# A graph network on one core: another order of the head's text, and the last load of x in two parts

## The chip, the core and the metric

The kernel runs on one core of one Trainium2 chip. Five engines work side by side, each on its own queue of instructions, in order: TensorE (PE, matmuls), VectorE (DVE), ScalarE (ACT), GpSimd (POOL) and SyncE (SP, which here only issues transfers). They wait for each other by semaphores. Sixteen DMA engines move data between HBM and the on-chip memory (SBUF); a transfer is issued from the queue of SP, ACT or POOL. Matmuls write to banks of PSUM, from which ACT and DVE copy results away. The metric is the time of one execution on the device, in microseconds (us); lower is better.

## What is computed

```python
h = jnp.maximum(_layernorm(x, axis=-1), 0.0)     # x: 2500 x 256
xs = [h]
for W, b in ((W0, b0), (W1, b1), (W2, b2)):      # W: 512 x 256
    xi, xj = h[dst], h[src]                      # 80000 edges, sorted by dst
    m = jnp.concatenate([xi, xj - xi], axis=-1) @ W + b
    s = jax.ops.segment_sum(m, dst, num_segments=N)
    cnt = jax.ops.segment_sum(ones, dst, num_segments=N)
    h = relu(s / jnp.maximum(cnt, 1.0)[:, None])
    xs.append(h)
out = x + jnp.concatenate(xs, axis=-1) @ Wf + bf
```

## The kernel before

The kernel turns the sums over edges into products with a matrix of counts: how often node `src` sends to node `dst`. x's 2500 rows lie in 20 tiles of 128 rows, taken as 10 pairs (pair q is tiles 2q and 2q+1). The columns of the count matrix are cut in windows of 6 nodes, and windows in batches of 4. Five groups of windows make the columns of one layer; the first layer's products of group g run while the counts of group g+1 are made, and layers 1 and 2 read the counts back from HBM.

This case is about the **head**, some 60 us in which x is normalized, the first products are made, edges are gathered and the counts of group 0 begin. Everything in it goes through a wrapper (`InOrder`, line 282, which therefore is the line of nearly all records) that keeps each engine's instructions in the order in which the program names them. That order is written out by hand in a string, `order` (lines 914 to 924): each word names an act, with a number for its pair, group, batch or window of keys, and `perform` calls them one after the other. An act puts its instructions at the end of the queues of the engines it uses; so two words may change places without any effect if they share no engine, and a word moved past another of the same engine changes that queue. The acts that matter here:

| word | what it does | engine |
| --- | --- | --- |
| `st` q | mean and variance of pair q's tiles (2 bn_stats, 2 bn_aggr), from x in `acc` | DVE |
| `rs`, `sq`, `sc` g | for a group of pairs: variance + eps; its root; the scale `rs` and offset `off` | DVE; ACT; DVE |
| `N` q | normalizes pair q in place in `acc`: pair 0 on DVE and ACT, 1 on ACT, from 2 on POOL | as told |
| `T`, `R` q | four transposes into the bank `turned`; relu of it into `hT` | PE; ACT |
| `Z`, `F` q | the pair's product with W's lower half, with Wf's first block, in a bank `pz` (each recorded as 8 matmuls) | PE |
| `H`, `L` q; `G` q | Z split into a high part `zh` and a low part `zl`; F copied to `acc` | ACT, DVE; ACT |
| `V` 9 | adds the bias row to the last tile's Z | DVE |
| `pk`, `sg`, `se` | find where each window's edges start: product, count of signs, position `start_i` (`se0` for keys 0, `se1` for keys 1 to 3) | PE; ACT; DVE |
| `ge` i | two indirect gathers of edges by `start_i`: `ed` (from dst), then `es` (from src) | POOL |
| `ka` i | `lo_i` from `es` (DVE); `away` from `ed` (ACT); a filter on `away` (DVE) | DVE, ACT |
| `km`, `kb` i | key parts `km` from `lo_i`; `kn` from `es` and `away` (two DVE instructions) | ACT; DVE |
| `kt`, `k1`, `k2` i | the keys transposed; copied to `key_m` and `key_n` | PE; ACT |
| `B` b | compares of keys with a row of numbers, for batches b and b+1 (a word whose batch is there already does nothing): one `one_m`, two `one_n` | DVE |
| `C` b, `E` b | counts of batch b in a bank (8 small matmuls, so that two batches are shown as 16); copied to `a` | PE; ACT |

The groups for `rs`, `sq` and `sc` are pairs 0; 1; 2 and 3; 4 to 7; 8 and 9. So `rs1`, `sq1` and `sc1` need only `st1`, and `sc2` needs `st2` and `st3`. B0 does only batch 0; B1, B3, B5, B7 and so on do two.

x comes in four chunks of tiles, 0 to 1, 2 to 5, 6 to 11 and 12 to 19, into `acc`. ACT's queue issues dst and then the chunk 6 to 11. SP's queue issues x 0 to 1, x 2 to 5, W's lower half (`wbf`, read by Z), x 12 to 19 (in two transfers, as the last tile has 68 rows), Wf's first block (`wbf`, read by F), W's upper half (`wt`, read after the head) and two short bias rows. The banks of `C`, `kt` and `pk` come from a pool of two, those of `T` from one of two, those of `Z` and `F` from one of four.

Of the kernel before, what the change touches and what calls it, by code (L numbers as in the profile page):

```python
# [10 lines left out]
AF = mybir.ActivationFunctionType  # L11
# [302 lines left out]
def by_windows(ctx: ExitStack, tc: tile.TileContext, x, src, dst, Ws, bs, Wf, bf, out, missing):  # L314
    nc = tc.nc
    PE, DVE, ACT, POOL, SP = nc.tensor, nc.vector, nc.scalar, nc.gpsimd, nc.sync
    PEo, DVEo, POOLo, ACTo, SPo = (InOrder(tc, e) for e in (PE, DVE, POOL, ACT, SP))
# [3 lines left out]
    NT = (N + P - 1) // P  # L321
# [15 lines left out]
    N1 = NT * KEEP  # L337
# [45 lines left out]
    away = early.tile([P, WG, CAP], BF16, name="away")  # L383
# [12 lines left out]
    lim = const.tile([P, WG], F32, name="lim")  # L396
    below = const.tile([P, WG], F32, name="below")
# [28 lines left out]
    def load_x(queue, a, b):  # L426
        queue.dma_start(acc[:, a:min(b, NT - 1), :], xr[:, a:min(b, NT - 1), :])
        if b == NT:
            queue.dma_start(acc[:LAST, NT - 1, :], x[(NT - 1) * P:N, :])

    chunks = [(0, 2), (2, 6), (6, 12), (12, NT)]
    load_x(SPo, *chunks[0])
    load_x(SPo, *chunks[1])
    load_x(ACTo, *chunks[2])
# [6 lines left out]
    def new_raw(l):  # L441
        raws[l] = raw_pools[-1].tile([P, DC, 2, D], F32, name="wbf", bufs=1)
# [8 lines left out]
    def load_wt(l, queue=SP):  # L451
        queue.dma_start(wts[l] if l == 1 else ws[l][0], Ws[l][0:D, :].rearrange("(c p) d -> p c d", p=P))

    def load_wf(l, queue=SP):
        if l == L:
            new_raw(l)
        wfs[l] = raws[l][:, :, 1, :]
        queue.dma_start(wfs[l], Wf[l * D:(l + 1) * D, :].rearrange("(c p) d -> p c d", p=P))

    load_wb(0, SPo)  # L460
    load_x(SPo, *chunks[3])
    load_wf(0, SPo)
    load_wt(0, SPo)

    lim_i = pp.tile([P, WG], I32, name="lim_i")
# [45 lines left out]
    first = pp.tile([P, 1], F32, name="first")  # L511
    after = pp.tile([P, 1], F32, name="after")
    behind = pp.tile([P, WG * P], F32, name="behind")
    pick = pp.tile([P, WG * P], F32R, name="pick")
# [7 lines left out]
    edges = [None] * WG  # L522
# [47 lines left out]
    def search(i, j):  # L570
        sl = slice(i, j)
        DVEo.tensor_add(base[:, 0, sl], base[:, 0, sl], base[:, 1, sl])
        DVEo.tensor_scalar(start_f[:, sl], row[:, sl], float(R), float(HR + P * R - MORE - CAP), op0=OP.mult, op1=OP.add)
        DVEo.scalar_tensor_tensor(start_f[:, sl], base[:, 0, sl], -0.5, start_f[:, sl], op0=OP.mult, op1=OP.add)
        DVEo.tensor_scalar(start_i[:, sl], start_f[:, sl], 0.0, float(E - CAP), op0=OP.max, op1=OP.min)
# [17 lines left out]
    parts = {}  # L593

    def key_parts(i):
        es, ed = edges[i]
        lo_i = pw.tile([P, CAP], I32, name="lo_i")
        DVEo.tensor_scalar(lo_i, es, P - 1, None, op0=OP.bitwise_and)

        ACTo.activation(away[:, i, :], ed, AF.Relu, bias=below[:, i:i + 1])  # L600
        DVEo.scalar_tensor_tensor(away[:, i, :P], away[:, i, :P], most if i == 0 else float(KEEP), away[:, i, :P],
                                  op0=OP.is_le, op1=OP.mult)
        parts[i] = [lo_i]

    def key_low(i):
        km = pw.tile([P, CAP], BF16, name="km")
        ACTo.copy(km, parts[i][0])
        parts[i][0] = km
# [18 lines left out]
    def key_copy(i, q):  # L627
        n = min(P, NW - i * P)
        to = (key_m, key_n)[q]
        ACTo.copy(to[:, i * P:i * P + n, :, :].rearrange("p n j r -> p j n r"),  # L630
                  parts[i][:, q * CAP:(q + 1) * CAP].rearrange("p (j n) -> p j n", j=CH)[:, :, :n]
                  .unsqueeze(3).to_broadcast([P, CH, n, REP]))
# [226 lines left out]
    def layer(l, g, a, own, PE=PE, ACT=ACT):  # L859
# [41 lines left out]
        "dstr": lambda: ACTo.copy(dst_r[:, MORE:], dst_i),  # L901
        "pk": lambda i: pick_half(i // 10, i % 10), "sg": lambda i: count_half(i // 10, i % 10),
        "se": lambda i: search(*((0, 1), (1, WG))[i]), "ge": get_edges,
        "ka": key_parts, "km": key_low, "kb": key_high, "kt": key_turn,
        "k1": lambda i: key_copy(i, 0), "k2": lambda i: key_copy(i, 1),
        "io": small_numbers, "ws": lambda: DVEo.tensor_sub(ws[0][0], ws[0][0], ws[0][1]),
        "st": stats, "rs": lambda g: spread(*groups[g]), "sq": lambda g: roots(*groups[g]),
# [4 lines left out]
        "warm": keep_warm,  # L912
    }
    order = """
        warm8 lim io first next dstr st0 rs0 sq0 pick sc0 warm7 N0 pk00 sg00 pk01 st1 T0 pk11 R0 sg01 st4 rs1 sq1 Z0 pk30 se0
        sg11 sc1 pk20 N1 st5 sg30 ge0 T1 st6 R1 F0 sg20 pk21 st7 pk10 H0 F1 rs3 st3 sq3 sc3 G0 st9
        L0 sg21 N6 pk31 ka0 kb0 Z1 N5 st8 N7 G1 T6 rs4 sg10 sg31 km0 T5 se1 kt0 R6 H1 st2 F6 sq4 sc4 k10 k20
        rs2 Z6 ge1 L1 T7 B0 R5 R7 Z5 B1 C0 B2 ka1 G6 H6 N9 H5 C1 T9 F7 E0 ge2 kb1 R9 sq2 km1 E1 kt1 C2 B3 k21 Z9
        k11 N8 L6 B4 E2 L5 C3 B5 C4 T8 E3 E4 C5 V9 R8 E5 ge3 ka2 H9 sc2 Z7 H7 F8 G7 B6 N3 N2 ka3 km2 T2 R2 km3
        kb2 C6 T3 kb3 B7 L7 kt2 Z2 B8 B9 L9 E6 C7 k22 k12 kt3 H2 N4 E7 B10 k13 k23 Z8 L2 C8 T4 C9 E8  # L920
        C10 H8 E9
        F9 B11 B12 C11 G8 E10 C12 R4 E12 E11 B13 F5 B14 C13 R3 B15 C14 E13 E14 L8 B16 Z3 G9 B17 C15 C16 H3 E15
        G5 B18 F3 C17 E16 C18 F4 E17 B19 C19 Z4 L3 G3 B20 E18 C20 B21 F2 E19 B22 H4 E20 L4 G4 B23 G2 B24 ws
# [29 lines left out]
    C1 = 1.0 + 1.0 / E12  # L953
# [483 lines left out]
def gnn_kernel(tc: tile.TileContext, x, src, dst, Ws, bs, Wf, bf, out):  # L1437
    nc = tc.nc
    with tc.tile_pool(name="flag", bufs=1) as flag:
        missing = flag.tile([1, 1], I32, name="missing")  # L1440
        tc.mark_branch_hint_location("again", "LikelyTaken",
                                     engines=[getattr(mybir.EngineType, e) for e in ("PE", "DVE", "Activation")])
        near_end = by_windows(tc, x, src, dst, Ws, bs, Wf, bf, out, missing)
        loads, (again,) = nc.values_load_multi_w_load_instructions(missing, min_val=0, max_val=1)

        for d in loads:
            if d.ins.engine in [getattr(mybir.EngineType, e) for e in ("PE", "DVE", "Activation")]:
                tc.add_manual_dep(d.ins, near_end.ins.name,
                                  mybir.DependencyInfo(mybir.DependencyClass.Sync, mybir.DependencyReason.DATA),
                                  reason="behind the outputs")  # L1450
        with tc.If(again > 0, label="again"):
            general(tc, x, src, dst, Ws, bs, Wf, bf, out)
# [28 lines left out]
```

## Time and profile before

| | us |
| --- | --- |
| median of 3 runs | 473.46 (473.29 to 473.58) |
| the profiled execution | 473.55 |
| its span, first to last record | 471.7 |
| PE busy from 8 to 20, 20 to 37, 37 to 61, 61 to 470 | 11.12, 16.84, 23.61, 405.40 |
| DVE busy in the same | 10.79, 14.07, 22.42, 326.92 |
| granted TensorE clock, mean | 0.998 |

The profile records one execution: for each instruction its start, its duration and the engine. Views: a page with busy times and a span in 40 slices; the chain of work that ended last, followed back from the end to what released each step; the waits by engine, with what ended them; the timeline in order of time, in which equal neighbours are merged; and the transfers. Matmuls are pipelined: each starts before the one ahead has ended, so the distance of starts tells PE's pace. Times below are us from the start of the span.

### The profile page before, as it was taken

To read this page: it belongs to the slowest core of one execution; us is meant where nothing else is said; L and a number is where in the kernel's file an instruction comes from. 1 tells how busy PE (TensorE), PEld (TensorE's weight loads), DVE (VectorE), ACT (ScalarE), POOL (GpSimd) and SP (SyncE) were. 2 spreads that over 40 slices of the span, in tenths; PEclk is the share of its full clock that TensorE was granted. 3 is DMA by queue.
4 is the path that set the end of the run, shared out by engine and by line. 5 is a ranking of instruction groups with operands and counts; after the bars stand their busy time and mean duration, and the time that the engine had idled before them with its cause. 6 is when DMAs were issued, how large, how long until landed. Compare 5 with 4: busy or idle time off the path is not lost.

```text
span 471.7 us, 7365 instructions
## 1 busy us (share of the span) xinstructions
PE 463.1 (98%) x2739; PEld 365.6 (77%) x2739; DVE 380.3 (81%) x699; ACT 310.5 (66%) x543; POOL 43.2 (9%) x66
## 2 busy tenths in 40 slices
PE   8999999999999999999999999999999999999995
PEld 3787888787878878877887877876788788688685
DVE  7988988799898873499987847877899687578795
ACT  4876677686664542368769867874787798397540
POOL 2684014300101001000000000000000000000000
PEclk9999999999999999999999999999999999999999
DMA  8310083991823707532168551110212955220014
GB/s 277 92 54 3 1 164 64 189 215 30 164 58 69 153 0 149 128 97 77 48 217 317 190 175 40 50 45 1 88 44 83 347 188 195 88 89 0 1 62 159
DMA packets 21775, 52.07 MB, mean 110 GB/s; under 512 B 1943, under 2 KB 12134, under 8 KB 21734
## 3 DMA queue, kind: packets, MB, share of 16 engines
q1 hardware_dynamic: 14374, 33.41, 21.6%
q0 software_dynamic: 5856, 16.51, 18.3%
q10 hardware_dynamic: 1504, 1.63, 1.1%
q8 instruction: 22, 0.36, 0.3%
q14 instruction: 19, 0.16, 0.1%
HBM read 36.08 MB, written 15.46 MB: 109 GB/s over the span
## 4 chain that ended last, share of the span: by engine, by line
PE 88%; DVE 5%; POOL 3%; DMA 2%; issue 1%; ACTq 0%; DVEq 0%; POOLq 0%
PE bank L282 84%; PE pz L282 3%; DMA acc<-in_x_dram 2%; DVE acc L282 2%; POOL acc L282 1%; DVE st L282 1%; POOL ed L282 1%; POOL es L282 1%; DVE staged L282 1%; DVE tmp L282 0%; DVE zl L282 0%; DVE mv L282 0%; PE turned L282 0%; DVE kn L282 0%; DVE rs L282 0%
## 5 line engine op out<-in xcount | busy, mean ns | idle before, releaser
L282 ACT CAST block<-staged 128x1008 fp32r<-128x1008 bf16 x120 | 117.8, 1031 | 17.1 <-DVE staged L282 6.3
L282 PE MATMUL bank<-block,zh 128*128 128x504 f32 (+1 forms) x200 | 83.7, 419 | 0.0
L282 PE MATMUL bank<-a,zh 128*128 128x504 f32 (+1 forms) x200 | 81.7, 409 | 0.0
L282 ACT CAST a<-bank 128x480 fp32r<-128x480 f32 (+1 forms) x105 | 54.4, 561 | 38.6 <-PE bank L282 36.9
L282 PE MATMUL bank<-a,zl 128*128 128x504 f32 (+1 forms) x200 | 77.8, 389 | 0.0
L282 PE MATMUL bank<-block,zl 128*128 128x504 f32 (+1 forms) x200 | 77.3, 387 | 0.0
L282 DVE TENSOR_TENSOR one_m<-iota_m,key_m 128x2048 bf16<-128x2048 bf16 (+2 forms) x55 | 64.3, 1169 | 9.9 <-PE bank L282 9.7
L282 PE MATMUL bank<-block,sh 128*128 128x504 f32 x160 | 69.0, 431 | 0.0
L282 PE MATMUL bank<-block,staged 128*128 128x512 f32 (+1 forms) x288 | 63.5, 371 | 0.3 <-DVE staged L282 0.2
L282 PE MATMUL bank<-block,sl 128*128 128x504 f32 x160 | 62.6, 391 | 0.0
L282 PEld LDWEIGHTS bank<-block,staged 128*128 128x128 f32 x288 | 49.2, 188 | 11.4 <-DVE staged L282 1.6
L282 DVE TENSOR_TENSOR one_n<-iota_n,key_n 128x960 bf16<-128x960 bf16 (+2 forms) x110 | 51.5, 509 | 0.0
L282 DVE TENSOR_TENSOR block<-staged 128x1008 fp32r<-128x1008 bf16 x40 | 47.0, 1205 | 5.5 <-PE bank L282 4.3
L282 PEld LDWEIGHTS <-one_m 128*128 128x128 bf16 x834 | 37.4, 97 | 13.4 <-issue 7.5
L282 PEld LDWEIGHTS bank<-block,zh 128*128 128x128 f32 x200 | 37.6, 188 | 10.8 <-issue 2.5
L282 PEld LDWEIGHTS bank<-block,zl 128*128 128x128 f32 x200 | 37.6, 188 | 10.6 <-issue 3.5
L282 PE MATMUL bank<-one_n,one_m 128*128 128x120 bf16 x834 | 44.7, 204 | 0.0
L282 PEld LDWEIGHTS bank<-a,zh 128*128 128x128 f32 x200 | 37.8, 189 | 6.4 <-issue 0.2
L282 PEld LDWEIGHTS bank<-a,zl 128*128 128x128 f32 x200 | 37.8, 189 | 6.3 <-issue 0.2
L282 DVE TENSOR_TENSOR staged<-staged 128x1008 bf16<-128x1008 bf16 x40 | 27.2, 679 | 17.3 <-ACT block L282 16.9
L282 PE MATMUL pz<-wbf,hT 128*128 128x256 f32 x160 | 38.7, 387 | 0.2 <-ACT hT L282 0.2
L282 PEld LDWEIGHTS bank<-block,sh 128*128 128x128 f32 x160 | 30.1, 188 | 10.4 <-issue 3.5
(163 smaller groups left out, 617.7 us busy)
## 6 DMA issues: line engine op xcount, KB each, us to landing
staged<-a_dram SPq DMA_DIRECT2D x52, 504.0 KB, 4.5
a_dram<-a POOLq DMA_DIRECT2D x20, 630.0 KB, 10.3
acc<-in_x_dram POOLq DMA_DIRECT2D x3, 640.0 KB, 14.3
out_dram<-acc SPq DMA_DIRECT2D x15, 128.0 KB, 1.8
wbf<-in_L_gnn_Wf_dram SPq DMA_DIRECT2D x4, 256.0 KB, 12.6
acc<-in_x_dram SPq DMA_DIRECT2D x1, 896.0 KB, 9.9
acc<-in_x_dram ACTq DMA_DIRECT2D x1, 768.0 KB
wbf<-in_L_gnn_W_dram SPq DMA_DIRECT2D x3, 256.0 KB, 7.2
```

Of the source, the lines that this page charges most:

```text
L282: return self.tc.keep_in_program_order(call(*args, **kwargs))
```

## The change

Four things change, all in the head. The last chunk of x is cut in two, tiles 12 to 15 and 16 to 19, and Wf's first block is loaded between them. The ACT part of `ka` becomes an act of its own, `aw`, so that it can stand elsewhere than its DVE part. In the order, `st2` comes ahead of `rs1`, where `st4` stood, and `st4` goes behind `sc1`. And from the fourth line of the order on: `sc2` and `aw2` go to the place behind B4, `ka2` and `kb2` right behind `V9`, `aw3` and `km2` ahead of `Z7`, `C6` between `Z7` and `F8`, `ka3` and `kb3` ahead of `H7`, `N2` ahead of `N3`, and T2 and T3 come to stand together behind `F8`. After `C8` nothing is changed.

```diff
-    chunks = [(0, 2), (2, 6), (6, 12), (12, NT)]
+    chunks = [(0, 2), (2, 6), (6, 12), (12, 16), (16, NT)]
...
     load_wb(0, SPo)
     load_x(SPo, *chunks[3])
     load_wf(0, SPo)
+    load_x(SPo, *chunks[4])
     load_wt(0, SPo)
...
     def key_parts(i):
-        es, ed = edges[i]
+        es = edges[i][0]
         lo_i = pw.tile([P, CAP], I32, name="lo_i")
         DVEo.tensor_scalar(lo_i, es, P - 1, None, op0=OP.bitwise_and)
-
-        ACTo.activation(away[:, i, :], ed, AF.Relu, bias=below[:, i:i + 1])
         DVEo.scalar_tensor_tensor(away[:, i, :P], away[:, i, :P], most if i == 0 else float(KEEP), away[:, i, :P],
                                   op0=OP.is_le, op1=OP.mult)
         parts[i] = [lo_i]
+
+    def find_away(i):
+        ACTo.activation(away[:, i, :], edges[i][1], AF.Relu, bias=below[:, i:i + 1])
...
-        "ka": key_parts, "km": key_low, "kb": key_high, "kt": key_turn,
+        "aw": find_away, "ka": key_parts, "km": key_low, "kb": key_high, "kt": key_turn,
...
-        warm8 lim io first next dstr st0 rs0 sq0 pick sc0 warm7 N0 pk00 sg00 pk01 st1 T0 pk11 R0 sg01 st4 rs1 sq1 Z0 pk30 se0
-        sg11 sc1 pk20 N1 st5 sg30 ge0 T1 st6 R1 F0 sg20 pk21 st7 pk10 H0 F1 rs3 st3 sq3 sc3 G0 st9
-        L0 sg21 N6 pk31 ka0 kb0 Z1 N5 st8 N7 G1 T6 rs4 sg10 sg31 km0 T5 se1 kt0 R6 H1 st2 F6 sq4 sc4 k10 k20
-        rs2 Z6 ge1 L1 T7 B0 R5 R7 Z5 B1 C0 B2 ka1 G6 H6 N9 H5 C1 T9 F7 E0 ge2 kb1 R9 sq2 km1 E1 kt1 C2 B3 k21 Z9
-        k11 N8 L6 B4 E2 L5 C3 B5 C4 T8 E3 E4 C5 V9 R8 E5 ge3 ka2 H9 sc2 Z7 H7 F8 G7 B6 N3 N2 ka3 km2 T2 R2 km3
-        kb2 C6 T3 kb3 B7 L7 kt2 Z2 B8 B9 L9 E6 C7 k22 k12 kt3 H2 N4 E7 B10 k13 k23 Z8 L2 C8 T4 C9 E8
+        warm8 lim io first next dstr st0 rs0 sq0 pick sc0 warm7 N0 pk00 sg00 pk01 st1 T0 pk11 R0 sg01 st2 rs1 sq1 Z0 pk30 se0
+        sg11 sc1 pk20 N1 st4 st5 sg30 ge0 T1 st6 R1 F0 sg20 pk21 st7 pk10 H0 F1 rs3 st3 sq3 sc3 G0 st9
+        L0 sg21 N6 pk31 aw0 ka0 kb0 Z1 N5 st8 N7 G1 T6 rs4 sg10 sg31 km0 T5 se1 kt0 R6 H1 F6 sq4 sc4 k10 k20
+        rs2 Z6 ge1 L1 T7 B0 R5 R7 Z5 B1 C0 B2 aw1 ka1 G6 H6 N9 H5 C1 T9 F7 E0 ge2 kb1 R9 sq2 km1 E1 kt1 C2 B3 k21 Z9
+        k11 N8 L6 B4 sc2 aw2 E2 L5 C3 B5 C4 T8 E3 E4 C5 V9 ka2 ge3 kb2 R8 E5 H9 aw3 km2 Z7 N2 N3 C6 ka3 kb3 H7 F8 G7 B6 T2 R2
+        km3 T3 E6 B7 L7 kt2 Z2 B8 B9 L9 C7 k22 k12 kt3 H2 N4 E7 B10 k13 k23 Z8 L2 C8 T4 C9 E8
```

## The prediction

> **What bounds it.** I read the busy table first, then the slices, then the chain of waits in order of time, then the waits and the timeline of the first 48 us.
>
> ```profile
> PE 463.1 (98%) x2739; PEld 365.6 (77%) x2739; DVE 380.3 (81%) x699; ACT 310.5 (66%) x543; POOL 43.2 (9%) x66
> PE   8999999999999999999999999999999999999995
> ```
>
> TensorE (PE) is busy in all slices but the first and the last, and the chain is PE from 37.76 to 132 us (but for 0.02 us) and nearly so to the end. The work after the head is the same in both kernels, and from 61 to 470 us PE is busy for 405.4 of 409 us. So the change is worth what it moves the moment from which PE never waits again. That moment in the chain, and what stands ahead of it:
>
> ```profile
> 32.91 0.97 POOL es L282
> 33.88 1.34 issue
> 35.27 2.44 POOL acc L282 x4
> 37.76 0.44 PE turned L282 x2
> ...
> 41.00 0.05 PE bank L282
> 41.07 0.66 PE bank L282 x11
> ```
>
> The second half of T2 (`turned`) starts at 37.76 behind POOL's normalization (`acc`), and C7 at 41.07 behind the compare B7. The waits of the first 48 us (engine, waited for, total, times, longest):
>
> ```profile
> DVE st L282 <- DMA acc<-in_x_dram: 1.0, 1, 1.0
> ...
> PEld pz L282 <- DMA wbf<-in_L_gnn_Wf_dram: 0.2, 1, 0.2
> ```
>
> and of DVE from 20 to 42 us:
>
> ```profile
> DVE lo_i L282 <- DMA es<-in_src_dram,start_i: 1.4, 1, 1.4
> DVE away L282 <- ACT away L282: 1.3, 1, 1.3
> ```
>
> PE's timeline from 7.7 to 41 us is its queue's own work but for these holes: about 2 us up to 13.60 (it follows N0, N1 and Wf), 0.4 to 21 us, 0.8 to 0.9 around T2 (F8 ends near 36.8, T2's half waits to 37.76), 0.2 before C7 and 0.14 at C11 (16 matmuls took 0.80 where the others take 0.66). Some 1.2 us near the end is therefore within reach, and of the 2 us at the start only what is not lost again.
>
> **The change, part by part.**
>
> *st2 for st4 ahead of rs1.* DVE sat idle from 9.17 to 10.18, for x rows that come on ACT's queue. st2 (2 x 0.33 and 0.22: 0.87 us, the row of a pair of bn_stats) needs only rows that st1 already had, so it fills the hole. rs1, se0 and sc1 no longer stand behind the load but behind sg01 on ACT (ends 10.14): sc1 ends at 11.05 instead of 11.98. ge0 and N1 start 0.9 earlier (N1 on ACT 11.1 to 12.2). st4 now follows sc1, ends at 11.95, where sc1 ended before: from st5 to se1 DVE is where it was, and ge1 starts at 21.05 as before. st2's old place behind se1 (20.71 to 21.59) is empty: 0.87 us less DVE ahead of L1 and B0.
>
> *The loads.* SP's queue has one more issue (0.5 us by its rows; nothing on SP waits for issues before the `brow` rows). 384 + 68 KB no longer stand ahead of Wf; at the 299 to 350 GB/s of the windows from 8 to 14 us that is 1.3 to 1.5 us, and Wf, which landed at 13.60 (the wait), lands near 12.2. The Trainium skill, "DMA: Bandwidth & Descriptors", section "Anatomy of one DMA", speaks against splitting: about 2.0 us fixed for each DMA. By that sum Wf, one DMA later than need be, would gain nothing. The windows show transfers run without gaps (DMA share 1.03 to 1.11 from 4 to 14 us), so a fixed part lies beside other transfers; I take the 1.4. x's last rows land when Wf did, about 13.6; st9, their first reader, is at 15.85: hidden by 2 us, and the last load (wt) isn't read before the head's end.
>
> *PE with both.* F0 starts behind T1 at 12.45 instead of 13.60. F1, Z1, T6, T5 follow as before (N6 is done at 17.13, N5 at 18.4); kt0 has to wait for kn of kb0 (19.18): 19.3 for 20.20; F6 19.5 for 20.61. So PE is 1.1 us ahead from 19.5 on: Z5 23.5, T9 25.95, F7 26.4.
>
> *DVE and POOL, 21 to 33 us.* B0 starts at 21.70 (k20 ends 21.55), B1 at 22.94, ending 25.05 to 25.35. es1 lands about 25.1 (2.7 after its issue), ka1 at 25.2 for 26.07, B3 26.5 for 27.33. sc2 (0.35, from 34.80) now comes between L6 and L5, so B5 starts at 30.05 for 30.55 and ends at 32.15. C5's last matmuls read B5: C5 ends at 32.45 for 33.12. **That cuts PE's lead to 0.67**: most of what the loads gave is lost again here.
>
> POOL shares something with DVE's compares:
>
> ```profile
> 26.57 1.03 POOL L282 DMA_INDIRECT ed<-in_dst_dram,start_i  x1 [0.16 <-issue]
> 27.90 1.49 POOL L282 DMA_INDIRECT es<-in_src_dram,start_i  x1 [0.30 <-issue]
> ...
> 30.67 1.94 POOL L282 DMA_INDIRECT ed<-in_dst_dram,start_i  x1 [0.16 <-issue]
> 32.91 0.97 POOL L282 DMA_INDIRECT es<-in_src_dram,start_i  x1 [0.30 <-issue]
> ```
> ```profile
> 27.33 1.22 DVE L282 TENSOR_TENSOR one_m<-iota_m,key_m 128x2048 bf16<-128x2048 bf16 x1
> 28.47 0.97 DVE L282 TENSOR_TENSOR one_n<-iota_n,key_n 128x960 bf16<-128x960 bf16 x2
> ...
> 30.55 1.22 DVE L282 TENSOR_TENSOR one_m<-iota_m,key_m 128x2048 bf16<-128x2048 bf16 x1
> 31.69 0.97 DVE L282 TENSOR_TENSOR one_n<-iota_n,key_n 128x960 bf16<-128x960 bf16 x2
> ```
>
> An indirect issue takes 0.97 alone; the two that began inside a one_m ended 0.92 after that one_m did (28.47, 31.69). Both tell that it stands still until the running compare ends. The Trainium skill, "SBUF — State Buffer", "Who interferes with whom", has the exclusive port of DVE and GpSimd, but says (as an inference) that a tensor_tensor doesn't stall the writing of descriptors. By that, moving compares would cost or give nothing at the issues; by the rows, an issue that begins inside one_m loses up to 1.2 us. I go by the rows, and every edit of DVE's times re-rolls these meetings. Laid out: es1 22.31 to 23.3 (was 23.31); N9 behind B1 to 25.7 (was 26.41); ed2 25.85; es2 27.15, held by B3 to 28.6 (was 29.39); N8 to 29.75; ed3 at 29.9 against B5's one_m at 30.05. If it begins first it ends at 30.9, es3 at 32.15; if not, 32.15 and 33.4 (was 33.88). es3's edges land 2.6 after: 34.75 or 36.0, was 36.5.
>
> *aw2, kb2, aw3 earlier.* Away2 held DVE 1.35 us (33.24 to 34.59); at its new place on ACT (29.4 to 29.85, ed2 landed about 29.2) it is done before DVE comes, and kb2 goes with it into the time before es3. Two ACT rows (0.5) move ahead of E2; C4 waits for E2's bank and still starts unhindered (E2 ends 30.35, C4 at 30.8). aw3, ahead of km2, H7, G7 and R2 in ACT's queue, waits for ed3's landing (2.36 after its issue ends: 34.97 less 32.61) at 33.3 to 34.5; R2 must be done at 37.5 and is, at 36.9 plus 0.6. If ed3 landed 1 us later still, R2 would be late. From es3's landing to B7 there remain lo_i, away, hi_i, kn: 1.45 us, where it was 2.17 (kb2's 0.75 is gone). B7 starts at 36.2 or 37.45, was 38.72.
>
> *sc2 early, C6 between Z7 and F8, T2 and T3 together.* N2, now ahead of N3 as T2 is of T3, and N3 no longer wait for sc2 (1.39): they run behind ge3, to 34.5 or 35.8. Z7 32.45, C6 34.25 (E4 is done), F8 34.6, T2 36.4, T3 36.9 to 37.35, both without a wait; kt2 at 37.35 for 38.83, Z2 37.6 to 39.4. C7 needs B7's end (start plus 2.2): 38.4 or 39.65. C7 at 39.4 or 39.65 for 41.02.
>
> **The sum.** Lead carried to C5's end 0.67, T2's stall 0.81, C7's 0.15, C11's 0.14: 1.75 at most; 1.35 where ed3 meets B5. After C7 both PE and DVE keep their distance, and nothing there waits. The meeting is a toss, and small excess waits on the way are likelier than none: I take 1.4. Span 471.7 - 1.4 = 470.3, and the 1.85 us around the span (profiled execution 473.55) give 472.15; the median of the runs lies 0.09 lower, so **472.1**.
>
> **The rivals.**
>
> 1. *The gate stays.* POOL's chain gains nothing, es3 lands at 36.5 as before; then only kb2's 0.75 is gone: B7 37.97, gain 0.77, **472.7**. For it: every POOL time above depends on a meeting. Against it: B1 and B3 end 0.85 earlier.
> 2. *The loads do nothing* (Wf lands no earlier, F0 at 13.60). PE comes to C5 as before, then 0.81, 0.15 and 0.14 remain: **472.4**. For it: the fixed cost above. Against: gapless transfers.
> 3. *Slower.* es1 (22.31) no longer begins 0.16 before B0 but inside it. If the compares keep the port from one to the next, as they kept N9's second half (24.18 to 26.41, 2.23 us for 0.55) through all of B1, es1 issues only at 25.05 and lands at 27.75: ka1 1.7 late, B3 at 29.0, B5 32.6, C5 ends 35.0 for 33.12. Of these 1.9 us the 0.81 at T2 and some 0.15 come back: +0.95, **474.4**. It decides from the point where es1 is held over 0.9 us. For it: N9's row. Against: es2 and ed3 did get in between one_m and one_n.
> 4. *Nothing*: another wait between 41 and 60 us takes the lead back, **473.5**; DVE is full there, but ahead.
>
> **Chances.** Forecast 0.50, rival 1 0.18, rival 2 0.10, rival 3 0.17, rival 4 0.05. About 0.2% (0.95 us) is what a measurement of this kernel can tell from no change. Faster by more: 0.49 of the forecast, 0.08 of rival 2, 0.03 of rival 1: 0.60. Slower by more: most of rival 3, 0.14. The rest, 0.26, within. The forecast's own range is 471.6 to 472.6; with the rivals 471.4 to 474.2 leaves out no more than the ends of rival 3 and gains over 2 us.
>
> **What would show it.** F0 at 12.4; se1 at the same time as before; B0 0.8 earlier; es1's issue about 1.0 us long (rival 3: over 2); C5's end 0.7 earlier; no wait of PE for POOL at T2; B7 at 36 to 37.5; PE at C7 1.4 to 1.6 ahead and so at the first `bank<-a,zh` (60.89 now). I am wrong if es3 lands after 36.5, if ACT stands at aw3 past 35.5, or if the lead at C7 is gone at 61 us.

## The result, and the profile after

| | before | after | after, timed again |
| --- | --- | --- | --- |
| median of the runs, us | 473.40 (473.20 to 473.58) | 471.70 (471.29 to 472.05) | 472.28 |
| ratio to before, 95% interval | | 0.9965 [0.9955, 0.9975] | 0.9977 [0.9968, 0.9986] |
| the profiled execution, its span | 473.55, 471.7 | 472.05, 470.2 | 472.28, 470.4 |

The changed kernel is faster, by 1.7 us in one timing and 1.3 in the other (there before took 473.54). The profiled execution took 472.05, where the sum gave 472.15. Such totals are too coarse for terms of 0.2 us: dst and x land some tenths earlier or later from one execution to the next, and the 410 us behind the head, which is the same code, took 410.8 before and 410.6 and 410.4 in two executions after. (That scatter lies in the tail: up to the start of PE's last matmul they took 405.51, 405.50 and 405.46.) So all that follows reads three starts on PE: the first `pk` (the first `bank<-dst_r,pick`), Z7 (the first `pz` behind C5), and the first `bank<-a,zh`. I call the time from `pk` to Z7 stretch A and that from Z7 to `bank<-a,zh` stretch B. Two executions of the changed kernel gave 25.13 and 25.09 for A, 26.84 and 26.81 for B, within 0.05 us of each other. Run 12 will show 0.13 in A that none of its edits explains, so a difference under 0.15 in these sums is not read as a gain. From `pk` on the change is worth 1.20 or 1.27 us, near the 1.3 of the second timing; the rest of the first timing's 1.7 is not explained by these rows.

| | A | B | A + B | against before |
| --- | --- | --- | --- | --- |
| before | 25.40 | 27.77 | 53.17 | |
| after | 25.13 | 26.84 | 51.97 | 1.20 less |
| forecast (most, sum of its terms) | 24.73 | 26.67 | 51.40 | 1.77 less |

The busy table of the changed kernel, and its chain of waits in order of time (start, us, what; only the longest pieces):

```profile
PE 462.6 (98%) x2739; PEld 365.7 (78%) x2739; DVE 380.8 (81%) x699; ACT 310.7 (66%) x543; POOL 41.4 (9%) x66
```
```profile
30.38 1.13 DVE one_m L282
31.51 0.90 DVE one_n L282 x2
32.45 0.44 PE bank L282 x7
32.89 1.81 PE pz L282 x8
...
36.84 0.87 PE turned L282 x8
37.96 1.99 PE pz L282 x8
```

PE's busy share has not moved; what moved is where the chain goes over to PE for the rest of the head: at 32.45 (C5), out of DVE's compare B5, where before it was at 37.76 (T2), out of POOL. T2 and T3 now run as one piece. PE's timeline of the same place (start, us, what, count):

```profile
32.13 0.75 PE L282 MATMUL bank<-one_n,one_m 128*128 128x120 bf16 x8
32.73 1.97 PE L282 MATMUL pz<-wbf,hT 128*128 128x256 f32 x8
34.53 0.49 PE L282 MATMUL bank<-one_n,one_m 128*128 128x120 bf16 x8
34.86 1.97 PE L282 MATMUL pz<-wbf,hT 128*128 128x256 f32 x8
36.67 1.04 PE L282 MATMUL turned<-shift,acc 128*128 128x128 f32 x8
37.55 0.28 PE L282 MATMUL bank<-ident_b,km 128*128 128x128 bf16 x2
37.66 0.28 PE L282 MATMUL bank<-ident_b,kn 128*128 128x128 bf16 x2
37.96 1.99 PE L282 MATMUL pz<-wbf,hT 128*128 128x256 f32 x8
39.79 0.49 PE L282 MATMUL bank<-one_n,one_m 128*128 128x120 bf16 x8
```

The reader is to see four things. C5 (32.13) takes 0.75 where a batch takes 0.49: PE has caught up with DVE's B5. Z7 starts at 32.73 for 33.12. T2, T3 and kt2 follow without a hole. And between kt2's second pair of transposes (37.66) and Z2 (37.96) there are 0.30 us where before there were 0.12: Z2 waits for R2, a hole that the prediction hadn't seen. PE's wait, and R2 on ACT:

```profile
PE pz L282 <- ACT hT L282: 0.2, 1, 0.2
```
```profile
37.31 0.60 ACT L282 ACTIVATE hT<-turned 128x512 f32<-128x512 f32 x1 [0.62 <-PE turned L282]
```

DVE and POOL of the same stretch:

```profile
28.56 0.68 DVE L282 TENSOR_TENSOR zl<-pz,zh 128x512 fp32r<-128x512 f32 x1
29.16 0.17 DVE L282 RECIPROCAL rs<-rs 128x4 f32<-128x4 f32 x1
29.36 0.41 DVE L282 SCALAR_TENSOR_TENSOR off<-mv,rs 128x4 f32<-128x4 f32 x1
29.70 0.68 DVE L282 TENSOR_TENSOR zl<-pz,zh 128x512 fp32r<-128x512 f32 x1
30.30 1.21 DVE L282 TENSOR_TENSOR one_m<-iota_m,key_m 128x2048 bf16<-128x2048 bf16 x1
...
35.99 0.29 DVE L282 TENSOR_SCALAR lo_i<-es 128x256 int32<-128x256 int32 x1 [1.99 <-DMA es<-in_src_dram,start_i]
...
37.60 1.21 DVE L282 TENSOR_TENSOR one_m<-iota_m,key_m 128x2048 bf16<-128x2048 bf16 x1
```
```profile
23.36 2.97 POOL L282 TENSOR_SCALAR acc<-acc,rs,off 128x256 f32<-128x256 f32 x2
...
29.20 1.09 POOL L282 TENSOR_SCALAR acc<-acc,rs,off 128x256 f32<-128x256 f32 x2
30.45 1.90 POOL L282 DMA_INDIRECT ed<-in_dst_dram,start_i  x1 [0.16 <-issue]
32.66 0.97 POOL L282 DMA_INDIRECT es<-in_src_dram,start_i  x1 [0.30 <-issue]
33.66 3.74 POOL L282 TENSOR_SCALAR acc<-acc,rs,off 128x256 f32<-128x256 f32 x6
```

`sc2` (29.16 and 29.36) sits between L6 and L5. Its second instruction took 0.41 where it takes 0.16 elsewhere; N8 ran on POOL beside it. ed3 began at 30.45, 0.15 inside B5's `one_m`, and took 1.90: the toss of the prediction fell on the worse side, es3 landed at 35.99, and B7 started at 37.60 (before 38.72). Nothing of this stopped PE.

### The profile page after: what moved, and what is told of

The parts are those of the page before. It is cut to its first block, busy times and chain, and to the rows that moved or that the text cites. A ratio compares the mean times of both kernels' runs of the same rounds, so it can differ in the third digit from the quotient of the medians.

```text
span 470.2 us, 7370 instructions
## 1 busy us (share of the span) xinstructions
PE 462.6 (98%) x2739; PEld 365.7 (78%) x2739; DVE 380.8 (81%) x699; ACT 310.7 (66%) x543; POOL 41.4 (9%) x66
## 4 chain that ended last, share of the span: by engine, by line
PE 89%; DVE 8%; DMA 1%; ACT 0%; issue 0%; DVEq 0%
PE bank L282 85%; PE pz L282 4%; DVE acc L282 2%; DVE st L282 1%; DVE one_m L282 1%; DMA acc<-in_x_dram 1%; DVE zl L282 1%; DVE one_n L282 1%; DVE staged L282 1%; DVE tmp L282 0%; DVE mv L282 0%; PE turned L282 0%; DVE kn L282 0%; DVE rs L282 0%; ACT junk L282 0%
## 5 line engine op out<-in xcount | busy, mean ns | idle before, releaser
L282 PEld LDWEIGHTS bank<-block,zh 128*128 128x128 f32 x200 | 37.6, 188 | 10.8 <-issue 2.5
L282 PEld LDWEIGHTS bank<-block,zl 128*128 128x128 f32 x200 | 37.6, 188 | 10.6 <-issue 3.5
## 6 DMA issues: line engine op xcount, KB each, us to landing
acc<-in_x_dram POOLq DMA_DIRECT2D x3, 640.0 KB, 11.9
```

The source lines that it names most:

```text
L282: return self.tc.keep_in_program_order(call(*args, **kwargs))
```

## The experiments

The theory: late edits (from `sc2` on) take T2's hole away; the early edits (`st2`, the loads) give PE and DVE a lead, of which DVE's order lets little through to C5. The rivals differ by run. Times of A and B are collected here; the ratios are against before, timed beside each, with their 95% intervals.

| kernel | A | B | A + B | ratio |
| --- | --- | --- | --- | --- |
| before | 25.40 | 27.77 | 53.17 | |
| 1 after, old loads | 25.82 | 26.64 | 52.46 | 0.9979 [0.9970, 0.9988] |
| 2 before, new loads | 25.27 | 27.77 | 53.04 | 0.9992 [0.9983, 1.0001] |
| 3 before, `st2` early | 25.38 | 27.75 | 53.13 | 0.9998 [0.9990, 1.0007] |
| 4 before, late part | 26.10 | 26.64 | 52.74 | 0.9981 [0.9972, 0.9990] |
| after | 25.13 | 26.84 | 51.97 | 0.9965 [0.9955, 0.9975] |
| 7 after, `sc2` behind V9 | 24.84 | 27.51 | 52.35 | 0.9980 [0.9971, 0.9989] |
| 7 again | 24.85 | 27.51 | 52.36 | 0.9977 [0.9966, 0.9987] |
| 8 as 7, B7 ahead of `ka3` | 25.52 | 27.39 | 52.91 | 0.9977 [0.9969, 0.9986] |
| 9 after again | 25.09 | 26.81 | 51.90 | 0.9977 [0.9968, 0.9986] |
| 10 after, N9 on ACT | 24.86 | 26.64 | 51.50 | 0.9968 [0.9957, 0.9980] |
| 11 as 10, `sc2` behind V9 | 24.59 | 26.64 | 51.23 | 0.9966 [0.9954, 0.9978] |
| 12 as 11, C6 behind T3 | 24.72 | 26.32 | 51.04 | 0.9954 [0.9941, 0.9968] |

### 1 to 4: the parts one by one

Run 1 takes the loads back out of the changed kernel:

```diff
-    chunks = [(0, 2), (2, 6), (6, 12), (12, 16), (16, NT)]
+    chunks = [(0, 2), (2, 6), (6, 12), (12, NT)]
...
-    load_x(SPo, *chunks[4])
```

> The new order with the old loads (x 12 to 19 in one piece, Wf behind it). Theory (what counts is when B5, T2 and C7 let PE go on): F0 is back near 13.6 and PE comes 1.1 us later to every step up to T9, but most of that lead was lost again at C5, which waits for B5; so PE leaves C5 only 0.3 to 0.4 later than in the changed kernel, span 470.5 to 470.6, 1.1 below before. Rival (the earlier Wf is the gain): 1.2 later than the changed kernel, span 471.4.

It was 0.49 behind after in A + B, a little more than the 0.3 to 0.4 of the theory and far from the rival's 1.2. F0 waited for Wf again, as PE's timeline says:

```profile
13.66 0.70 PE L282 MATMUL pz<-wbf,hT 128*128 128x256 f32 x2 [1.05 <-DMA wbf<-in_L_gnn_Wf_dram]
```

PE was 1.3 us later as far as T9 (27.14 for 25.82), but B5 only 0.76. What carried the delay to DVE is ACT: with the transposes and copies later, DVE's `rs` stood behind ACT's root, in the order of the queue.

```profile
21.22 0.18 DVE L282 RECIPROCAL rs<-rs 128x4 f32<-128x4 f32 x1 [0.54 <-ACT rs L282]
```

In A the loads are worth 0.69 (25.82 less 25.13), and 0.20 of it is lost in B. Of these, 0.14 is C11, whose 16 matmuls took 0.66 in run 1 (from start to the next start) and 0.80 in after:

```profile
46.16 0.82 PE L282 MATMUL bank<-one_n,one_m 128*128 128x120 bf16 x16
```
```profile
45.46 0.96 PE L282 MATMUL bank<-one_n,one_m 128*128 128x120 bf16 x16
```

PE comes to it later in run 1, and DVE earlier, because ed3 began ahead of B5 (31.06) there and wasn't held:

```profile
30.68 0.97 POOL L282 DMA_INDIRECT ed<-in_dst_dram,start_i  x1 [0.16 <-issue]
```
```profile
36.70 1.21 DVE L282 TENSOR_TENSOR one_m<-iota_m,key_m 128x2048 bf16<-128x2048 bf16 x1
```

This B7 is 0.90 ahead of that of after, and so the loads also decided, in these executions, how ed3's toss fell.

Runs 2 and 3 put one early part alone into the kernel before: the chunks and loads, and the order of `st2` and `st4`.

```diff
-        ... pk11 R0 sg01 st4 rs1 sq1 Z0 pk30 se0
-        sg11 sc1 pk20 N1 st5 ...            ... H1 st2 F6 ...
+        ... pk11 R0 sg01 st2 rs1 sq1 Z0 pk30 se0
+        sg11 sc1 pk20 N1 st4 st5 ...        ... H1 F6 ...
```

> The old order with the new loads alone. Theory: Wf lands near 12.2, but F0 stands behind T1, whose second half waits for N1, which ends near 13.1; F0 moves by 0.2 at most and the time by 0 to 0.2 (span 471.5 to 471.7). Rival (the earlier Wf is the gain): 1.2 less, span 470.5.

> The old order with st2 ahead of rs1 and st4 behind sc1 alone (old loads, old places of sc2, away, kb2, T2, T3). Theory: DVE is 0.87 ahead from L1 on, but PE gets nothing of it: F0 waits for Wf, C5 is bound by PE itself, T2 still waits for N2 behind sc2, and B7 for es3 and kb2. Gain 0 to 0.3, span 471.4 to 471.7. Rival (each 0.87 of DVE comes through to the end, since DVE bounds C7): span 470.8.

They gave 0.13 and 0.04, no more than the scatter. In run 2 F0 started at 13.61 although Wf was there: it followed T1, which followed N1 on ACT. In run 3 it started at 13.75 and waited 0.93 for Wf. Either part alone leaves F0 where it was, as the other one's reason takes over; with both it starts at 12.39. Where two things end at nearly the same time, removing one shows nothing.

Run 4 is the other side: the kernel before with all edits from `aw` and `sc2` on, without `st2` and the loads.

> The old order up to B4 and the old loads, the new order behind it (sc2, aw2, kb2, aw3, C6, T2 and T3 at their new places). Theory: T2's hole (0.81) and C7's and C11's waits (0.3) go, but B5 comes 0.5 later behind sc2, so C5 loses 0.3: gain 0.8, span 470.9. Rival (the late part is only as good as the lead that the early part gives): gain 0 to 0.2, span 471.5.

It gave 0.43, where 0.8 had been expected, and the two stretches say why: B fell by 1.13, with T2's, C7's and C11's waits gone, but A grew by 0.70, because `sc2` now stands ahead of B5 on DVE: from B3 to B5 it took 3.72 for 3.22 (`off`, beside N8, 0.37). The early part and the loads then take 0.97 out of A again (26.10 to 25.13) and lose 0.20 in B. So the 1.20 isn't a sum of independent parts: 0.04 + 0.13 + 0.43 make half of it. Two reasons are on record: each early part alone leaves F0 in its place, and the late part puts DVE work ahead of B5, for which it needs the lead (`st2` is worth 0.04 alone and 0.28 beside the late part: 52.74 less 52.46). How the missing half divides between the two isn't shown: no run has both early parts without the late one.

### 5: the gather against a compare

The prediction rested on rows that began inside a compare. Run 5 is a small kernel of its own, which leaves the network out: POOL runs 4 gathers or 6 `tensor_scalar` (as N does), while DVE runs nothing, then compares like `one_m`, then subtractions from PSUM like L.

> Not the network: x is copied to the output, and beside it GpSimd issues four indirect gathers, and later six tensor_scalar of 128x256, each against three things on DVE: nothing, 16 compares of the form of one_m back to back, 16 to 24 subtractions with one operand in PSUM. Theory (an issue that begins inside a compare stands still until that compare ends): a gather's issue is 1.0 us alone and against PSUM subtractions, up to 2.2 against compares, and the compares go on in between. Rival A (a compare with two SBUF operands doesn't stall the writing of descriptors): 1.0 in all three. Rival B (compares back to back keep the port): the first gather ends only after the last compare, some 18 us. For tensor_scalar the theory says 0.55 alone and against PSUM, and 1 to 2.2 against compares.

POOL's timeline: four gathers against compares, then six `tensor_scalar` alone, against compares, and against subtractions (some small copies that order the phases are left out).

```profile
10.06 1.91 POOL L30 DMA_INDIRECT ed<-in_dst_dram,start_i  x1
12.28 0.95 POOL L30 DMA_INDIRECT ed<-in_dst_dram,start_i  x1 [0.30 <-issue]
13.53 0.95 POOL L30 DMA_INDIRECT ed<-in_dst_dram,start_i  x1 [0.30 <-issue]
14.78 0.95 POOL L30 DMA_INDIRECT ed<-in_dst_dram,start_i  x1 [0.30 <-issue]
...
46.38 3.23 POOL L30 TENSOR_SCALAR hs<-hs,rs 128x256 f32<-128x256 f32 x6
...
51.08 9.07 POOL L30 TENSOR_SCALAR hs<-hs,rs 128x256 f32<-128x256 f32 x6
...
71.58 3.23 POOL L30 TENSOR_SCALAR hs<-hs,rs 128x256 f32<-128x256 f32 x6
```

The first gather began inside the compare from 9.90 to 11.12 and ended 0.85 after it; ed3 in the changed kernel began inside B5's `one_m` and ended at 32.35, 0.84 after it (31.51). The next three came 0.10 to 0.12 before a compare's end and took 0.95, as alone (0.95 to 1.16), though more compares followed at once. So an issue that begins inside a compare is held to the end of that compare, and is not held to the last of a chain; its remaining 0.85 ran beside the next compare, which took its usual 1.22: the form of rival 3 in which all compares of a chain hold it is excluded for gathers. POOL's arithmetic pays more: 1.51 us each for 0.54, and the compares that were met took 1.46 for 1.22 (one of them 1.38). Subtractions that read PSUM cost neither side anything (gathers 0.94 to 0.97, arithmetic 3.23, subtractions 0.69 met or not).

### 7 and 8: the term that came out too small

A's lead was 0.27 for 0.67 forecast. Run 7 moves `sc2` out from between L6 and L5, so that B5 starts 0.47 earlier (0.58 counted from `pk`).

```diff
-        k11 N8 L6 B4 sc2 aw2 E2 L5 ... C5 V9 ka2 ge3 ...
+        k11 N8 L6 B4 aw2 E2 L5 ... C5 V9 sc2 ka2 ge3 ...
```

> The changed kernel with sc2 moved from between L6 and L5 to behind V9. Theory: B5 starts 0.54 earlier, C5's wait for B5 (0.5) goes, ed3 begins inside B5's one_m still and ends 0.5 earlier, es3 and B7 too; gain 0.4 to 0.5 over the changed kernel, span 469.7 to 469.8. Rival (C5's wait is made up later, since B7 bounds C7): the same span as the changed kernel, 470.2.

A miss: A fell by 0.29 and B rose by 0.67. The repetition says the same.

> sc2 behind V9 again, beside the changed kernel. Theory: sc2's place between L6 and L5 is cover for N8, which POOL finishes there before B5's one_m starts; without it B5 starts 0.5 earlier, holds N8's second half (2.6 for 1.09), T8 and all of ge3 come later, B7 0.5 later: 0.4 to 0.6 us slower than the changed kernel. Rival (the difference of the first runs came from the chip or the moment): the same time, or 0.4 faster.

POOL's timeline of run 7:

```profile
29.27 2.63 POOL L282 TENSOR_SCALAR acc<-acc,rs,off 128x256 f32<-128x256 f32 x2
32.05 0.97 POOL L282 DMA_INDIRECT ed<-in_dst_dram,start_i  x1 [0.16 <-issue]
33.33 1.03 POOL L282 DMA_INDIRECT es<-in_src_dram,start_i  x1 [0.31 <-issue]
```

B5, at 29.83, now catches N8, which needs 2.63 for 1.09; T8 waits for it (0.90 long for 0.63), so that A keeps only 0.29. ed3 and es3 go 1.6 and 0.7 later, lo_i waits 2.79 for es3, B7 starts at 38.09, and C7 waits again (39.93, 0.75 for 0.49): 0.31 ahead of it, 0.26 in it and 0.09 behind kt3 make B's 0.67. In the changed kernel the row of `sc2` and L5 were cover for N8. I had priced the DVE time that the move saves and not who runs on POOL in it.

Run 8 tries to take B7 out of that chain, by putting B7 ahead of the last key's parts.

```diff
-        ... C6 ka3 kb3 H7 F8 G7 B6 T2 R2
-        km3 T3 E6 B7 L7 kt2 ...
+        ... C6 H7 F8 G7 B6 T2 R2
+        T3 E6 B7 ka3 kb3 km3 L7 kt2 ...
```

> As the one with sc2 behind V9, and B7 ahead of ka3 and kb3, so that DVE doesn't stand 2.0 us for es3 before it. Theory: B7 then runs from 34.0 to 36.2 just where POOL has N2 and N3, holds them, and T2 or T3 waits for POOL 0.3 to 0.9 us: no better than the kernel with sc2 moved alone, up to 0.5 slower. Rival (POOL isn't held): C7 and C11 don't wait for DVE any more, 0.15 faster than it.

B7 did run behind kb2 (35.44), but there it met N2 to N4, 5.92 us for 3.74 in after, and both halves of T3 stood waiting for POOL:

```profile
38.95 0.44 PE L282 MATMUL turned<-shift,acc 128*128 128x128 f32 x2 [0.21 <-POOL acc L282]
39.64 0.44 PE L282 MATMUL turned<-shift,acc 128*128 128x128 f32 x2 [0.25 <-POOL acc L282]
```

As the rival had it, C7 and C11 no longer wait for DVE (0.49 and 0.66), but T2 and T3 now take most of that back: B is 0.12 less than in run 7, within the scatter, and 0.55 more than in after. (In this execution the head itself began later, `pk` at 8.58 and ge1 at 22.54, so A isn't to be compared.)

### 9 to 12: without the meeting

Run 9 is the changed kernel again, timed beside run 7 again and runs 10 and 11.

> The changed kernel once more, to be timed on the same chip as the two runs beside it. Theory: 0.9965 of the kernel before, within its interval 0.9955 to 0.9975, and ed3 caught again by B5's one_m (1.9 for 0.97).

ed3 was caught again (1.90), and A and B came out as before; the ratio, 0.9977, lies just outside the interval of the first timing.

Run 10 takes from POOL the work that meets B1: N9 goes to ACT, which waits there 1.74 us for T7's bank.

```diff
-            elif q >= 2:
+            elif 2 <= q < 9:
...
-        rs2 Z6 ge1 L1 T7 B0 R5 R7 Z5 B1 C0 B2 aw1 ka1 G6 H6 N9 H5 ...
+        rs2 Z6 ge1 L1 T7 B0 R5 N9 R7 Z5 B1 C0 B2 aw1 ka1 G6 H6 H5 ...
```

> The changed kernel with pair 9 normalized on ACT behind R5, where ACT stands 1.7 us for T7, instead of on POOL, where N9 takes 3.0 us against B1. Theory: ge2 starts 3 us earlier, B1's one_m is no longer held (0.4 on DVE), T9's wait (0.2) and part of C5's go, ed3 and es3 come 1 us earlier or more: 0.4 to 0.6 us faster than the changed kernel. Rival (POOL's chain doesn't matter any more, or N9 on ACT holds R7 and what follows): the same or slower.

Up to the first `bank<-a,zh` it was 0.40 to 0.47 shorter than the two runs of after; the medians of the timed runs differ by 0.12 (472.16 and, for run 9, 472.28), for which see below. DVE and POOL:

```profile
30.05 1.22 DVE L282 TENSOR_TENSOR one_m<-iota_m,key_m 128x2048 bf16<-128x2048 bf16 x1
...
34.57 0.29 DVE L282 TENSOR_SCALAR lo_i<-es 128x256 int32<-128x256 int32 x1 [0.32 <-DMA es<-in_src_dram,start_i]
```
```profile
26.05 3.02 POOL L282 TENSOR_SCALAR acc<-acc,rs,off 128x256 f32<-128x256 f32 x2
29.23 0.98 POOL L282 DMA_INDIRECT ed<-in_dst_dram,start_i  x1 [0.16 <-issue]
```

B1's `one_m` took 1.21 for 1.64, `off` 0.16 for 0.41, and B5 started at 30.05. N8 is met now (3.02, by B3), but early enough; ed3 begins ahead of B5 and takes 0.98, es3 has landed at 34.57, and B7 starts at 35.73. A is 0.27 shorter, and in B C11's wait is gone (0.66): it followed DVE's compares behind B7. Run 11 adds the edit of run 7, which lost 0.4 there:

> N9 on ACT and sc2 behind V9. Theory: with N8 done before B5 comes, sc2's old place is no cover for anything, and C5's wait for B5 goes entirely: 0.2 to 0.4 us faster than N9 on ACT alone, span 469.4. Rival (N8 is still caught, by B3 or B5): no faster than it.

Now that N8 is done by 29.46 there is nothing for B5 to catch, and the same edit gains 0.27, all of it in A. C5's wait for B5 had been expected to go entirely; its row is still 0.75 (31.98). Run 12 also moves C6 into the hole ahead of Z2.

```diff
-        ... Z7 N2 N3 C6 ka3 kb3 H7 F8 G7 B6 T2 R2
-        km3 T3 E6 B7 ...
+        ... Z7 N2 N3 ka3 kb3 H7 F8 G7 B6 T2 R2
+        km3 T3 C6 E6 B7 ...
```

> The best version so far (N9 on ScalarE, sc2 behind V9) with one more edit: C6 stands behind T3 instead of between Z7 and F8. Only PE's order changes. Theory: with T2 and T3 both behind F8, kt2 and then Z2 come right behind T3 and Z2 has to wait for R2 (ScalarE), which cost 0.18 us more than before the change; with C6 (some 0.75 us) in that place the wait is gone, and the stretch from the first pick to the first bank of a and zh is 0.15 to 0.2 us shorter than the 51.23 of that version. Rival: Z2's wait has cover anyway (PE is caught later by C7 or C11) and the stretch stays within 0.05 of 51.23; if T2, now 0.6 us earlier, meets N2 or C7 meets B7, it is longer by up to 0.6.

```profile
36.91 0.49 PE L282 MATMUL bank<-one_n,one_m 128*128 128x120 bf16 x8
37.24 0.27 PE L282 MATMUL bank<-ident_b,km 128*128 128x128 bf16 x2
37.35 0.28 PE L282 MATMUL bank<-ident_b,kn 128*128 128x128 bf16 x2
37.47 1.95 PE L282 MATMUL pz<-wbf,hT 128*128 128x256 f32 x8
```

Z2 follows kt2 by 0.12, as before the change, and A + B is 0.19 shorter than in run 11. The sum is as expected; of its terms B gives 0.32, and A, which the edit doesn't touch, is 0.13 longer. Run 12 is the best: 2.13 us under before in A + B, 0.9 under after; its ratio is 0.9954, though its interval overlaps that of after's first timing and touches that of the second, so that the timed runs alone don't tell them apart.

A + B overstates runs 10 to 12. From the first `bank<-a,zh` to the start of PE's last matmul, before, after and runs 1 to 4 and 7 to 9 all took 405.46 to 405.51 us, but runs 10, 11 and 12 took 405.81, 405.75 and 405.78. The 0.3 us go at the passage from the first layer to the second, near 207 us, where a later load of Wf lands later, counted from the head's end. ACT's row that waits for it, in after and in run 10, and PE's in run 10:

```profile
191.83 1.06 ACT L282 ACTIVATE block<-wbf 128x1024 fp32r<-128x1024 f32 x1 [8.09 <-DMA wbf<-in_L_gnn_Wf_dram]
```
```profile
191.73 1.06 ACT L282 ACTIVATE block<-wbf 128x1024 fp32r<-128x1024 f32 x1 [8.43 <-DMA wbf<-in_L_gnn_Wf_dram]
```
```profile
206.54 2.60 PE L282 MATMUL bank<-block,staged 128*128 128x512 f32 x10 [0.23 <-DVE staged L282]
```

In after PE runs these matmuls without a wait. Why the load lands later in the runs with N9 on ACT is open. Counted from `pk` to PE's last matmul, run 10 is 0.05 to 0.16 under the two executions of after, run 11 0.38 to 0.49, and run 12 0.54 to 0.65 (1.86 under before).

## Why the prediction was right, point by point

The time lay in the range and the kind of gain came as forecast. That 1.4 came near the measured 1.20 (from `pk`) owes something to luck: the first term was 0.40 too large, and the discount of 0.37, taken for the toss and for waits not named, nearly made up for it.

**The kind of gain was right.** PE no longer waits for POOL at T2, C7 runs without a wait, and the chain leaves DVE and POOL five us earlier. The terms, in the order of the sum:

| term | forecast | measured | from |
| --- | --- | --- | --- |
| lead carried to C5's end | 0.67 | 0.27 | A: 25.40 less 25.13 |
| T2's stall | 0.81 | 0.89 | Z7 to kt2: 5.71, 4.82 |
| (Z2 waits for R2) | 0 | -0.18 | kt2 to Z2: 0.23, 0.41 |
| C7 and kt3 | 0.15 | 0.22 | Z2 to Z8: 2.61, 2.39 |
| C11's wait | 0.14 | 0 | 0.80 in both |
| sum | 1.77 at most (the text has 1.75), 1.35 if ed3 meets B5, 1.4 taken | 1.20 | |

**The mis-sized term** is the first. The forecast had B5 at 30.05; it began at 30.30, and as the head of this execution began 0.12 earlier (`pk` 7.60 for 7.72), that is 0.37 late. Some 0.25 of it is the row `off`, priced at 0.16 and measured at 0.41 beside N8 (0.38 and 0.37 in runs 1 and 4, where N8 ran there too), the rest B1's `one_m`, which N9 held for 1.64 (1.50 before). The same meeting held N9 to 26.33 where the text had 25.7, and so ed3 began at 30.45 for 29.9. Run 10, which takes N9 away, has both at their price and B5 at 30.05. So the sum was right for a DVE that POOL leaves alone; the text counted what compares do to POOL and not what POOL does to DVE.

**The unforeseen term** is Z2's wait. I wrote Z2 at 37.6, with kt2 and R2 both done, and had R2 begin 0.5 behind T2's start; it began 0.64 behind (37.31 and 36.67). With T3 and kt2 drawn up right behind T2, PE was ready for Z2 before R2 ended at 37.91. Run 12 puts cover there and the wait goes.

**C11** didn't gain, as PE and DVE both came 1.1 to 1.3 us earlier (C11 at 45.46 for 46.78, B7 at 37.60 for 38.72) and kept their distance. Its 0.14 belonged to the branch of the toss that didn't come: in runs 1, 4, 10, 11 and 12, where ed3 began ahead of B5, the 16 matmuls took 0.66, and in before and in runs 2, 3 and 9, where it was caught, 0.80.

**The early steps** were right: `st2` fills the hole, F0 starts at 12.39 (12.45), kt0 at 18.88 and its second pair, which needs kn, at 19.07 (19.3), F6 at 19.34 (19.5), and from st5 to ge1 (20.91) DVE is where it was but for the earlier start. Wf, issued at 3.04, landed 8.9 us later, near 11.9, where the sum by the windows' rate had 12.2; F0 was bound by T1, so its start doesn't measure the landing. The argument for rival 2 was wrong in itself: the split leaves Wf one transfer less to stand behind, not one more, so a fixed part for each transfer, such as the Trainium skill states ("DMA: Bandwidth & Descriptors", "Anatomy of one DMA": about 2.0 us, measured there on GpSimd's path, where these loads go out on SP), speaks for the split if for anything. That most of PE's lead is lost at B5 was right too, and more of it was lost than I said: 1.15 at T9, counted from `pk`, became 0.27.

**ed3's toss** fell as the second branch had it: 36.0 for es3 (35.99), 37.45 for B7 (37.60). The row that decided it, an issue held to the end of the running compare, is confirmed by run 5. I read the Trainium skill ("SBUF — State Buffer", "Who interferes with whom") as if compares left issues alone; it infers that only for the writing of descriptors, and has a DVE instruction with two SBUF inputs contend with a GpSimd instruction that reads SBUF. The rows don't contradict that: only the beginning of an issue was held, and its last 0.85 us ran beside a compare. Whether it is the reading of `start_i` that was held no run shows. aw3 waited until 34.91, past the forecast 34.5 and inside the time allowed (35.5).

**The rivals.** 1 (the gate stays) is out: es3 half a us earlier and PE not waiting. 2 (the loads do nothing) is out by F0 and by run 1, which puts them at 0.49 beside the other edits, though run 2 shows that alone they do next to nothing. 3 (es1 held through a chain of compares) didn't happen: es1's issue took 1.14. Run 7 shows that its kind was a real risk: the same sort of meeting, on N8 instead of es1, cost 0.4 us. 4 is out: the lead of 1.20 was still there at `bank<-a,zh`, and at PE's last matmul; but its kind exists, as the 0.3 us of runs 10 to 12 show, well behind 61 us. Of the signs that the text named, PE's lead at `bank<-a,zh` was missed (1.32 by the clock of the span, 1.20 from `pk`, for 1.4 to 1.6), as were C5's end (0.4 earlier for 0.7) and, by 0.1, B7 (37.60).

## What to carry to other kernels

Where several edits of an order are made together, time them alone and together, and read two stretches rather than the total: here three parts worth 0.04, 0.13 and 0.43 us gave 1.20, because the early parts hide each other's effect at F0, and the late part puts DVE work ahead of a compare and needs the lead that they make. Follow a gain to the end as well: of what runs 10 to 12 had won by 61 us, 0.3 was gone at 207. Price a moved instruction on a shared port by what runs on the other engine at its new time, in both directions: the same move of `sc2` lost 0.4 us where it uncovered POOL's work and gained 0.27 where that work had been moved away. And when two waits on PE are drawn together, look for what had stood between them and covered a third.

## What was not expected of the hardware

POOL's arithmetic slows the compares that it meets (1.46 for 1.22 in run 5, 1.64 for B1's) and even a 128x4 row (0.41 for 0.16), and is itself slowed nearly threefold (1.51 for 0.54), while neither pays against subtractions from PSUM. An indirect issue that begins inside a compare is held only to that compare's end, and then runs beside the next one. In run 5 POOL's `tensor_scalar` got in about once in each compare. In the changed kernel N9's two instructions took 2.97 us, from 23.36 to 26.33, past the end of B1's last `one_n` (25.26). Why they were held longer there than one compare each is not settled; no run took B1's chain apart.
